# Reordering the features of a pairwise attention on the chip, and summing three score slots in ten

## The chip, the cores and the metric

The kernel runs on one core of a Trainium2 chip. A core has a matrix engine (PE, with a weight loader shown as PEld), a vector engine (DVE), an activation engine (ACT), a general engine (POOL) and a queue engine that issues most transfers (SP). Each runs its own list of instructions in order and waits on semaphores for the others. The metric is the time of one execution in microseconds of device time; lower is better.

## The reference, cut to what matters

x has 64 graphs of 256 nodes with 128 features, adj is one 256x256 matrix. Each of four layers normalizes x, applies relu and adds a graph block's result to x: a gated recurrent block of five steps, a polynomial block, a block with normalized rows, and a pairwise attention. The change touches the last:

```python
def _L3_gnn_ref(x, W, b_lin, a, bias):           # called with W = bias = adj
    W1, W2 = (W[:, :F], W[:, F:])
    s1 = jnp.einsum('bkf,ef->bke', x, W1)
    s2 = jnp.einsum('bkf,ef->bke', x, W2)
    pre = s1[:, :, None, :] + s2[:, None, :, :] + b_lin
    h = jnp.where(pre >= 0, pre, ALPHA * pre)
    e = jnp.einsum('bije,e->bij', h, a) + bias
    attn = jax.nn.softmax(e, axis=2)
    out = jax.nn.sigmoid(jnp.einsum('bij,bjf->bif', attn, x))
```

For every graph and every pair (i, j) of its nodes, 256 features e are passed through a leaky relu and summed with weights a[e]. That is 64 x 256 x 256 x 256 values, and most of the time goes there.

## The kernel before

**Fronts and tails.** The graphs are taken two at a time: 32 pairs. `front(p)` is the chain of all work of a pair up to its attention: the first three layers and then the projections s1 and s2 of the fourth, in two halves of 128 features each, already multiplied by 0.8 times the size of a: s1a and the negated s2 in a PSUM bank (`s2a`, copied to `s2c`) for the first half, s1b and `s2n` for the second. `front` also makes `lin`, the linear part of the score that depends on j alone: a product with `g2`, copied as `quarter`, written to DRAM and read back over all partitions by two transfers on SP (L635, L637). `tail(p, ic, ...)` takes the finished scores of 128 nodes i, adds adj (L679, DVE) and lin (L689, POOL), and does softmax, the product with x, the sigmoid and the store.

**Slots, halves, tiles.** The leaky relu is a linear part plus a relu, and relu(s1 + s2) = s1 - min(s1, -s2), so a half is a min, or a relu, of one column of s1 (fixed i) against a row of s2 (all j). A slot is four nodes i, 32 apart; a pair has 64 slots, and each slot has two halves. One half of one slot fills one tile `rl`, 128 features x 4 nodes x 2 graphs x 256 nodes j (128x2048). Three engines fill tiles, one whole tile each at a time, in `work_on_tile`: DVE takes the first half with one min of 2048 columns (L794); ACT takes the second half with eight relus of 256 columns (L808); POOL takes either half with eight instructions of 256 columns (L820), whose scalar s1 comes through one pointer while the other operand is a constant.

**Scoring and summing.** PE sums over the 128 features: `score` multiplies a tile with a 128x32 window of `win` or `win_n`, which holds a's sign in one column, so that the four nodes' sums go to four rows of a PSUM bank (four matmuls, L876). 64 such half-slots of tiles make a block of 128 nodes i. For one slot in four (`SHARE = (1, 4)`) the two halves are summed ahead of PE: DVE or POOL fills the first half, POOL fills the second half in a form with signs (L817: `s2z`, the second half's s2 times `rho`, the product of the two halves' signs, with two pointers `s1h` and `s1l` as lower and upper limits), and a transfer on POOL's queue adds the one tile into the other in SBUF (L837, 1 MB). PE then scores one tile in place of two. `s2z`, `s1h` and `s1l` are made in the front by POOL (L647) and DVE (L660, L661).

**Order.** Every engine's order is fixed when the program is built, by a planner at the end of the kernel: it holds a planned clock for each engine, takes the engine whose clock is lowest, and gives it the ready piece with the best rank: a tail's step first, then a front's step, then an add or a score, then a new tile. Planned durations stand in the code. There are 12 tiles; an engine may hold at most 8 (DVE), 3 (ACT) and 4 (POOL) at once. The set-up of constants is two such chains; the second, `other_constants`, runs beside the first front.

Of the kernel before, what the change touches and what calls it, by code (L numbers as in the profile page):

```python
# [8 lines left out]
F32 = mybir.dt.float32  # L9
# [15 lines left out]
SHARE = (1, 4)  # L25
# [6 lines left out]
def kernel(  # L32
# [87 lines left out]
    def take():  # L120

        spare.sort(key=lambda b: b[1])
        return spare.pop(0)
# [36 lines left out]
    make_identity(nc, ident)  # L160
    minus_half = const.tile([P, NB * NC], F32, name="minus_half")
# [43 lines left out]
    win = const.tile([P, NE, 63], F32, name="win")  # L205
    win_n = const.tile([P, NE, 63], F32, name="win_n")
    w1 = const.tile([P, N], F32, name="w1")
    w2n = const.tile([P, N], F32, name="w2n")
    g2 = const.tile([P, 32], F32, name="g2")
    signs = const.tile([P, NE + 2], F32, name="signs")  # L210
    rho, never = signs[:, NE:NE + 1], signs[:, NE + 1:NE + 2]
# [47 lines left out]
    def other_constants():  # L259
# [22 lines left out]
        a_rep = work.tile([P, NE, P], F32, name="a_rep", tag="short", bufs=12)  # L282
        nc.vector.memset(a_rep, 1.0)
        for k in range(NE):
            nc.vector.tensor_scalar(a_rep[:, k, :], a_rep[:, k, :], acol[:, k:k + 1], None, op0=OP.mult)
        t_a = ran(DVE, 0.9)
        yield DVE, clock[DVE]
        nc.vector.memset(win, 0.0)
        nc.vector.memset(win_n, 0.0)
        nc.vector.tensor_scalar(signs[:, 0:NE], acol, 0.0, None, op0=OP.is_ge)  # L290
        nc.vector.tensor_scalar(signs[:, 0:NE], signs[:, 0:NE], 2.0, -1.0, op0=OP.mult, op1=OP.add)
        nc.vector.tensor_mul(rho, signs[:, 0:1], signs[:, 1:2])
        nc.vector.tensor_scalar(never, rho, MOST_NEGATIVE, None, op0=OP.mult)
        size = work.tile([P, NE], F32, name="size")
        nc.vector.tensor_mul(size, acol, signs[:, 0:NE])
        nc.vector.tensor_scalar(size, size, 1.0 - ALPHA, None, op0=OP.mult)
        nc.vector.tensor_mul(blin_s, blin, size)
        adj_s = work.tile([P, NE, N], F32, name="adj_s", tag="short", bufs=12)
        for k in range(NE):
            nc.vector.tensor_copy(win[:, k, 31:32], signs[:, k:k + 1])  # L300
            nc.vector.tensor_scalar(win_n[:, k, 31:32], signs[:, k:k + 1], -1.0, None, op0=OP.mult)
            nc.vector.tensor_scalar(adj_s[:, k, :], adj_n[:, k, :], size[:, k:k + 1], None, op0=OP.mult)
        t = ran(DVE, 2.4)
        for c in range(NC):
            yield PE, t, 1
            b = take()
            for k in range(NE):
                nc.tensor.transpose(b[0][:, k * P:(k + 1) * P], adj_s[:, k, c * P:(c + 1) * P], ident)
            t = ran(PE, 0.4, t, b[1])
            yield DVE, t  # L310
            if c:
                nc.vector.tensor_scalar(w2n, b[0][:, 0:N], -1.0, None, op0=OP.mult)
            else:
                nc.vector.tensor_copy(w1, b[0][:, 0:N])
            t = ran(DVE, 0.35, t)
            spare.append([b[0], t])

        yield PE, t_a, 1
        b = take()
        for k in range(NE):  # L320
            nc.tensor.matmul(b[0][:, 0:P], adj_n[:, k, P:2 * P], a_rep[:, k, :], start=(k == 0), stop=(k == NE - 1))
        t = ran(PE, 0.8, t_a, b[1])
        yield DVE, t
        nc.vector.tensor_scalar(g2, b[0][:, 0:32], ALPHA, None, op0=OP.mult)
        t = ran(DVE, 0.25, t)
# [97 lines left out]
    def front(p):  # L423
# [201 lines left out]
        for g in range(4):  # L625
            nc.tensor.matmul(b[0][g * 32:(g + 1) * 32, 0:P], g2, flat(hT)[:, g * P:(g + 1) * P],
                             start=True, stop=True, skip_group_check=True)
        t = ran(PE, 0.22, t_hT, b[1])
# [3 lines left out]
        t = ran(ACT, 0.2, t)  # L632
# [3 lines left out]
        lin = feat("lin")  # L636
        nc.sync.dma_start(flat(lin).rearrange("p (q n) -> p q n", q=4), row[0:P:32, :].unsqueeze(0).to_broadcast([P, 4, P]))  # L637
        t_lin = moved(moved(t))
# [6 lines left out]
        yield POOL, t_2  # L645
        s2z = feat("s2z")
        nc.gpsimd.tensor_scalar(s2z, s2n, rho, 1.0, op0=OP.mult, op1=OP.mult)  # L647
        t_z = ran(POOL, 0.65, t_2)
# [9 lines left out]
        yield DVE, t_b  # L658
        s1h, s1l = feat("s1h"), feat("s1l")
        nc.vector.tensor_scalar(s1h, s1b, never, None, op0=OP.max)  # L660
        nc.vector.tensor_scalar(s1l, s1b, -1.0, never, op0=OP.mult, op1=OP.min)  # L661
        t_z = max(t_z, ran(DVE, 1.0, t_b))
# [9 lines left out]
        READY[p] = dict(x3=x3, h3=h3, hT=hT, s1=(s1a, s1b), s2a=by_feature(s2a), s2c=s2c, s2n=s2n, s2z=s2z, s1h=s1h, s1l=s1l,  # L672
                        lin=lin, t_lin=t_lin, since=(max(t_n, t_s2a), max(t_b, t_2), t_z))

    def tail(p, ic, pe, since, x3, h3):

        yield DVE, since
        sc = feat("sc", **SHORT)
        nc.vector.tensor_add(sc, by_feature(pe), adj_n[:, ic, :].unsqueeze(1).to_broadcast([P, NB, N]))  # L679
        t = t_pe[p * NC + ic] = ran(DVE, ELEMENTS, since)  # L680
        ops = READY[p]
# [53 lines left out]
    tiles = [[relu_pool.tile([P, 4, NB, N], F32, name=f"rl{k}", bufs=1), 0.0] for k in range(12)]  # L735
# [43 lines left out]
    def work_on_tile(e):  # L779
# [10 lines left out]
        if e == DVE:  # L790
            since = max(ops["since"][k], free)
            whole = [P, 4, NB, N]
            rows = ops["s1"][0][:, :, i0:i0 + 97:32].rearrange("p b g -> p g b").unsqueeze(3)
            nc.vector.tensor_tensor(t, rows.to_broadcast(whole), ops["s2a"].unsqueeze(1).to_broadcast(whole), op=OP.min)  # L794
            done = ran(DVE, 2.2, since)
            t_s2v[p % 2] = max(t_s2v[p % 2], done)
            parts = 1
        elif e == ACT:
            since = max(ops["since"][k], free)
            if "s2p" not in ops:  # L800
                ops["s2p"] = s2p
                nc.scalar.copy(s2p, ops["s2n"])
                ran(ACT, COPY, since)
            parts = 2
            for g in (2 * part, 2 * part + 1):
                for b in range(NB):
                    i = i0 + g * 32
                    nc.scalar.activation(t[:, g, b, :], s2p[:, b, :], AF.Relu, bias=ops["s1"][1][:, b, i:i + 1], scale=-1.0)  # L808
            done = ran(ACT, 1.43, since)
        else:  # L810
            since = max(ops["since"][k], free)
            parts = 4
            for b in range(NB):
                i = i0 + part * 32
                row = slice(i, i + 1)
                if k == 2:
                    nc.gpsimd.tensor_scalar(t[:, part, b, :], ops["s2z"][:, b, :], ops["s1h"][:, b, row], ops["s1l"][:, b, row],  # L817
                                            op0=OP.min, op1=OP.max)
                else:
                    nc.gpsimd.tensor_scalar(t[:, part, b, :], ops["s2n" if k else "s2c"][:, b, :], ops["s1"][k][:, b, row],  # L820
                                            MOST_NEGATIVE, op0=OP.min, op1=OP.max)
            done = ran(POOL, 1.06 if k == 2 else 0.9, since)
# [40 lines left out]
    def score(tile_):  # L863
# [10 lines left out]
        w = win[:, 1] if e == ACT else win_n[:, k % 2]  # L874
        for g in range(4):
            nc.tensor.matmul(pe[g * 32:(g + 1) * 32, :], w[:, 31 - r:63 - r], flat(t[:, g]),  # L876
                             start=first, stop=(left[block] == 0), skip_group_check=True)
# [118 lines left out]
```

## Time and profile before

| What | us |
|---|---|
| Median of three runs (4946.7 to 4952.7) | 4949.8 |
| The profiled execution | 4947.9 |
| Its span | 4946.1 |
| Idle time of PE in the span (4946.1 - 4800.8) | 145.3 |
| Idle time of DVE | 193.5 |
| Idle time of ACT | 221.1 |
| Idle time of POOL | 231.6 |
| Start of the first tile (timeline) | 121.9 |
| Adds on POOL's queue, median from issue to landing | 7.6 |

The page gives for each engine its busy time, which is the union of its instructions' intervals; consecutive instructions overlap, so the mean duration of one is more than what one more would cost. A group of instructions is one line, engine and operation with its tiles: how many, their busy time, the mean of one, and the idle time before them with what ended it. PE's records are matmul passes: a matmul in float32 has two. L12 is line 12 of the kernel. The chain that ended last follows the work back from the last instruction, at each step to what released it.

### The profile page before, as it was taken

To read this page: it belongs to the slowest core of one execution; us is meant where nothing else is said; L and a number is where in the kernel's file an instruction comes from. 1 tells how busy PE (TensorE), PEld (TensorE's weight loads), DVE (VectorE), ACT (ScalarE), POOL (GpSimd) and SP (SyncE) were. 2 spreads that over 40 slices of the span, in tenths; PEclk is the share of its full clock that TensorE was granted. 3 is DMA by queue.
4 is the path that set the end of the run, shared out by engine and by line. 5 is a ranking of instruction groups with operands and counts; after the bars stand their busy time and mean duration, and the time that the engine had idled before them with its cause. 6 is when DMAs were issued, how large, how long until landed. Compare 5 with 4: busy or idle time off the path is not lost.

```text
span 4946.1 us, 132376 instructions
## 1 busy us (share of the span) xinstructions
PE 4800.8 (97%) x51993; PEld 1737.4 (35%) x51993; DVE 4752.6 (96%) x3302; ACT 4725.0 (96%) x12361; POOL 4714.5 (95%) x8918
## 2 busy tenths in 40 slices
PE   7999999999999999999999999999999999999997
PEld 3333333333333333333333333333333333333322
DVE  3999999999999999999999999999999999999998
ACT  3999999999999999999999999999999999999998
POOL 1999999999999999999999999999999999999998
PEclk9999999999999999999999999999999999999999
DMA  0556555565555565555565555655555555555566
GB/s 20 111 117 126 117 109 119 116 125 119 119 117 119 116 125 118 118 114 114 118 123 120 117 116 118 124 117 117 120 117 118 121 118 116 117 118 117 122 125 125
DMA packets 134051, 573.96 MB, mean 116 GB/s; under 512 B 12720, under 2 KB 67888, under 8 KB 67888
## 3 DMA queue, kind: packets, MB, share of 16 engines
q0 software_dynamic: 73728, 536.90, 54.2%
q1 hardware_dynamic: 58976, 28.59, 2.3%
q8 instruction: 406, 6.65, 0.5%
q14 instruction: 221, 1.81, 0.1%
q10 hardware_dynamic: 720, 0.00, 0.0%
HBM read 18.09 MB, written 10.49 MB: 6 GB/s over the span
## 4 chain that ended last, share of the span: by engine, by line
PE 52%; DVE 19%; POOL 14%; issue 5%; DMA 5%; ACT 4%; POOLq 0%; ACTq 0%; DVEq 0%
PE bank L876 32%; PE bank L338 18%; DVE rl L794 15%; POOL rl L817 6%; DMA rl<-rl 5%; POOL rl L820 5%; ACT rl L808 3%; PE bank L366 2%; POOL rl L837 1%; POOL d L505 1%; DVE hT L512 1%; DVE bank L508 1%; PE bank L359 1%; POOL mv L333 0%; DVE rh L470 0%
## 5 line engine op out<-in xcount | busy, mean ns | idle before, releaser
L808 ACT ACTIVATE rl<-bank,s1b 128x256 f32<-128x256 f32 x10344 | 4199.2, 947 | 63.3 <-PE bank L876 46.1
L794 DVE TENSOR_TENSOR rl<-s1a,bank 128x2048 f32<-128x2048 f32 x1844 | 4120.1, 2275 | 46.0 <-PE bank L876 22.9
L876 PE MATMUL bank<-rl,win_n 128*32 128x512 f32 x18328 | 2290.8, 594 | 78.3 <-DVE rl L794 53.9
L817 POOL TENSOR_SCALAR rl<-s2z,s1h,s1l 128x256 f32<-128x256 f32 x4096 | 2228.1, 634 | 13.2 <-PE bank L876 7.6
L876 PE MATMUL bank<-rl,win 128*32 128x512 f32 x10344 | 1367.4, 594 | 0.0
L876 PEld LDWEIGHTS bank<-rl,win_n 128*32 128x32 f32 x18328 | 580.4, 110 | 1320.4 <-issue 981.5
L820 POOL TENSOR_SCALAR rl<-s2n,s1b 128x256 f32<-128x256 f32 x1944 | 890.0, 521 | 18.5 <-DMA rl<-rl 3.5
L820 POOL TENSOR_SCALAR rl<-s2c,s1a 128x256 f32<-128x256 f32 x1632 | 747.4, 523 | 8.8
L876 PEld LDWEIGHTS bank<-rl,win 128*32 128x32 f32 x10344 | 335.9, 110 | 667.2 <-issue 529.0
L837 POOL DMA_DIRECT2D rl<-rl x512 | 413.3, 810 | 20.9 <-DVE rl L794 15.8
L338 PE MATMUL bank<-mT,wts 128*32 128x512 f32 x2560 | 335.3, 592 | 0.6 <-DVE rh L470 0.6
L338 PE MATMUL bank<-adj_t,h 128*32 128x256 f32 x5120 | 310.1, 383 | 3.6 <-ACT h L524 3.6
L505 POOL TENSOR_TENSOR d<-d,hT 128x512 f32<-128x512 f32 x155 | 206.8, 1334 | 58.9 <-ACT d L501 58.9
L338 PEld LDWEIGHTS bank<-adj_t,h 128*32 128x32 f32 x5120 | 165.3, 111 | 170.5 <-issue 53.8
L408 ACT ACTIVATE h<-x,mv 128x128 f32<-128x128 f32 x384 | 186.8, 795 | 7.3 <-DVE mv L404 6.8
L414 ACT COPY mT<-bank 128x512 f32<-128x512 f32 x160 | 153.3, 961 | 41.4 <-PE bank L338 39.7
L466 ACT ACTIVATE bank<-bank,gate_b 128x512 f32<-128x512 f32 x160 | 160.1, 1001 | 18.3 <-PE bank L338 15.5
L489 ACT ACTIVATE bank<-bank,gate_b 128x512 f32<-128x512 f32 x160 | 168.8, 1055 | 7.5 <-PE bank L338 7.5
L338 PE MATMUL bank<-rh,u5t 128*32 128x512 f32 x1280 | 168.3, 593 | 5.9 <-DVE rh L470 5.8
L501 ACT ACTIVATE d<-bank,gate_b 128x512 f32<-128x512 f32 x155 | 165.4, 1067 | 7.0 <-PE bank L338 6.8
L338 PE MATMUL bank<-mT,w 128*32 128x512 f32 x1280 | 168.3, 593 | 0.0
L338 PE MATMUL bank<-hT,wts 128*32 128x512 f32 x1280 | 168.1, 593 | 0.0
(132 smaller groups left out, 3476.1 us busy)
## 6 DMA issues: line engine op xcount, KB each, us to landing
rl<-rl POOLq DMA_DIRECT2D x512, 1024.0 KB, 7.6
xin<-in_x_dram SPq DMA_DIRECT2D x64, 128.0 KB, 6.1
lin<-row SPq DMA_DIRECT2D x32, 256.0 KB, 8.0
out_dram<-o SPq DMA_DIRECT2D x64, 128.0 KB, 3.6
row<-quarter SPq DMA_DIRECT2D x32, 64.0 KB, 4.1
w_raw<-in_L_gnn_w_w_dram SPq DMA_DIRECT2D x3, 128.0 KB, 2.8
th_raw<-in_L_gnn_Theta_dram SPq DMA_DIRECT2D x1, 320.0 KB, 3.7
adj_n<-in_adj_dram SPq DMA_DIRECT2D x1, 256.0 KB, 3.3
```

Source lines behind the costliest of these rows:

```text
L338: nc.tensor.matmul(o[g:g + 32], w[:, g:g + 32], t, start=start, stop=stop, skip_group_check=True)
L408: nc.scalar.activation(h[:, k, :], s[:, k, :], AF.Relu, bias=mv[:, k, 0:1], scale=mv[:, k, 1:2])
L466: nc.scalar.activation(r[0], pr[0], AF.Tanh, bias=br, scale=0.5)
L489: nc.scalar.activation(pr[0], pr[0], AF.Tanh, bias=bz, scale=0.5)
L501: nc.scalar.activation(d, by_feature(pv[0]), AF.Tanh, bias=bh, scale=1.0)
L505: nc.gpsimd.tensor_sub(d, d, hT)
L794: nc.vector.tensor_tensor(t, rows.to_broadcast(whole), ops["s2a"].unsqueeze(1).to_broadcast(whole), op=OP.min)
L808: nc.scalar.activation(t[:, g, b, :], s2p[:, b, :], AF.Relu, bias=ops["s1"][1][:, b, i:i + 1], scale=-1.0)
L817: nc.gpsimd.tensor_scalar(t[:, part, b, :], ops["s2z"][:, b, :], ops["s1h"][:, b, row], ops["s1l"][:, b, row], op0=OP.min, op1=OP.max)
L820: nc.gpsimd.tensor_scalar(t[:, part, b, :], ops["s2n" if k else "s2c"][:, b, :], ops["s1"][k][:, b, row], MOST_NEGATIVE, op0=OP.min, op1=O ...
L837: nc.gpsimd.dma_start(out=t.rearrange("p g b n -> p (g b n)"), in_=z.rearrange("p g b n -> p (g b n)"), accum_op=OP.add)
L876: nc.tensor.matmul(pe[g * 32:(g + 1) * 32, :], w[:, 31 - r:63 - r], flat(t[:, g]), start=first, stop=(left[block] == 0), skip_group_check= ...
```

## The change

`other_constants` now sorts the 256 features on the chip: those with a >= 0 first in their order, then the others from the end. Two iotas, comparisons and small matmuls with ones give each feature a rank; a 0/1 matrix `moved_to` per half, made by comparing the rank with a counter, sends the feature of rank 2m to the first half and that of rank 2m + 1 to the second, both at place m. So partners in the two halves share the sign of a, but for one pair when the number of positive features is odd; the one feature that then stands alone with the other sign, `odd`, is taken out of the sorted weights and is worked on by itself. The transposes of adj that gave `w1` and `w2n` become matmuls with `moved_to`.

As partners share their sign, a summed second half needs no rho and no two limits: POOL fills it with the same one-pointer instruction as any other tile. `s2z`, `s1h` and `s1l` are gone, and `win` and `win_n` have one half only.

The odd feature is a term min(s2o, s1o) for each pair of nodes. `front` makes s2o together with lin (one more column in `g2`'s matmul, a second broadcast transfer, ahead of that of lin) and s1o by four matmuls of one column and one small activation. The tail's first instruction, DVE's sum with adj, becomes two instructions (one for each graph) that add min(s2o, s1o) to the bank; adj is instead put into the bank by PE, by matmuls with the identity ahead of a block's first score.

The share of summed slots goes from one in four to three in ten, and the number of tiles from 12 to 13.

```diff
-SHARE = (1, 4)
+SHARE = (3, 10)
...
+    place = work.tile([P, N], mybir.dt.int32, name="place", bufs=1)
+    nc.gpsimd.iota(place, pattern=[[1, N]], base=0, channel_multiplier=0)
+    feature = work.tile([P, NE], mybir.dt.int32, name="feature", bufs=1)
+    nc.gpsimd.iota(feature, pattern=[[P, NE]], base=0, channel_multiplier=1)
...
-    win = const.tile([P, NE, 63], F32, name="win")
-    win_n = const.tile([P, NE, 63], F32, name="win_n")
+    win = const.tile([P, 63], F32, name="win")
+    win_n = const.tile([P, 63], F32, name="win_n")
...
+    odd_one = const.tile([P, 34], F32, name="odd_one")
+    g2, w1_odd, b_odd = odd_one[:, 0:32], odd_one[:, 32:33], odd_one[:, 33:34]
...
+        nc.vector.tensor_scalar(rest, number, total, None, op0=OP.add)
+        nc.vector.tensor_sub(rest, rest, counted)
+        nc.vector.tensor_sub(rank, counted, rest)
+        nc.vector.tensor_mul(rank, rank, positive)
+        nc.vector.tensor_add(rank, rank, rest)
...
+        moved_to = work.tile([P, NE, NE, P], F32, name="moved_to", tag="short", bufs=12)
+        for k in range(NE):
+            nc.vector.tensor_scalar(moved_to[:, k].rearrange("p h m -> p m h"), placed.rearrange("p (m h) -> p m h", h=NE),
+                                    rank[:, k:k + 1], None, op0=OP.is_equal)
...
             for k in range(NE):
-                nc.tensor.transpose(b[0][:, k * P:(k + 1) * P], adj_s[:, k, c * P:(c + 1) * P], ident)
-            t = ran(PE, 0.4, t, b[1])
+                nc.tensor.matmul(b[0][:, 0:N], adj_s[:, k, c * P:(c + 1) * P], moved_to[:, k].rearrange("p h m -> p (h m)"),
+                                 start=(k == 0), stop=(k == NE - 1))
+            t = ran(PE, 1.2, t, b[1])
...
+            nc.tensor.matmul(b[0][:, P + g:P + g + 1], flat(hT)[:, g * P:(g + 1) * P], w1_odd, start=True, stop=True)
...
+        s1o = work.tile([P, NB * NC], F32, name="s1o")
+        nc.scalar.activation(s1o, b[0][:, P:P + NB * NC], AF.Identity, bias=b_odd, scale=1.0)
...
-        nc.sync.dma_start(flat(lin).rearrange("p (q n) -> p q n", q=4), row[0:P:32, :].unsqueeze(0).to_broadcast([P, 4, P]))
-        t_lin = moved(moved(t))
+        lin, s2o = feat("lin"), feat("s2o")
+        for k, o in enumerate((s2o, lin)):
+            nc.sync.dma_start(flat(o).rearrange("p (q n) -> p q n", q=4), row[1 - k:P:32, :].unsqueeze(0).to_broadcast([P, 4, P]))
+            t = moved(t)
+        t = moved(t)
+        t_lin = t
...
-        s2z = feat("s2z")
-        nc.gpsimd.tensor_scalar(s2z, s2n, rho, 1.0, op0=OP.mult, op1=OP.mult)
...
-        s1h, s1l = feat("s1h"), feat("s1l")
-        nc.vector.tensor_scalar(s1h, s1b, never, None, op0=OP.max)
-        nc.vector.tensor_scalar(s1l, s1b, -1.0, never, op0=OP.mult, op1=OP.min)
...
-        nc.vector.tensor_add(sc, by_feature(pe), adj_n[:, ic, :].unsqueeze(1).to_broadcast([P, NB, N]))
-        t = t_pe[p * NC + ic] = ran(DVE, ELEMENTS, since)
+        for b in range(NB):
+            nc.vector.scalar_tensor_tensor(sc[:, b, :], ops["s2o"][:, b, :], ops["s1o"][:, b * NC + ic:b * NC + ic + 1],
+                                           by_feature(pe)[:, b, :], op0=OP.min, op1=OP.add)
+        t = t_pe[p * NC + ic] = ran(DVE, 0.8, since, ops["t_lin"])
...
-    tiles = [[relu_pool.tile([P, 4, NB, N], F32, name=f"rl{k}", bufs=1), 0.0] for k in range(12)]
+    tiles = [[relu_pool.tile([P, 4, NB, N], F32, name=f"rl{k}", bufs=1), 0.0] for k in range(13)]
...
-                if k == 2:
-                    nc.gpsimd.tensor_scalar(t[:, part, b, :], ops["s2z"][:, b, :], ops["s1h"][:, b, row], ops["s1l"][:, b, row],
-                                            op0=OP.min, op1=OP.max)
-                else:
-                    nc.gpsimd.tensor_scalar(t[:, part, b, :], ops["s2n" if k else "s2c"][:, b, :], ops["s1"][k][:, b, row],
-                                            MOST_NEGATIVE, op0=OP.min, op1=OP.max)
-            done = ran(POOL, 1.06 if k == 2 else 0.9, since)
+                nc.gpsimd.tensor_scalar(t[:, part, b, :], ops["s2n" if k else "s2c"][:, b, :], ops["s1"][min(k, 1)][:, b, row],
+                                        MOST_NEGATIVE, op0=OP.min, op1=OP.max)
+            done = ran(POOL, 0.9, since)
...
-        w = win[:, 1] if e == ACT else win_n[:, k % 2]
+        if first:
+            for b in range(NB):
+                side_by_side(by_feature(pe)[:, b, :], ident, adj_n[:, ic, :], b == 0, False)
+            ran(PE, 0.87, since, t_pe.get(block - 2, 0.0))
+        w = win if e == ACT else win_n
         for g in range(4):
             nc.tensor.matmul(pe[g * 32:(g + 1) * 32, :], w[:, 31 - r:63 - r], flat(t[:, g]),
-                             start=first, stop=(left[block] == 0), skip_group_check=True)
+                             start=False, stop=(left[block] == 0), skip_group_check=True)
```

## The prediction

> **What bounds the kernel now.** I read the busy line of the page first, then the chain that ended last, the costliest groups, the windows by stage, the timeline and the waits. The profiled execution took 4947.9 us (span 4946.1); the median of the three timed runs is 4949.8, so a sum made against the one is good for the other within 2 us.
>
> ```profile
> PE 4800.8 (97%) x51993; PEld 1737.4 (35%) x51993; DVE 4752.6 (96%) x3302; ACT 4725.0 (96%) x12361; POOL 4714.5 (95%) x8918
> ...
> PE 52%; DVE 19%; POOL 14%; issue 5%; DMA 5%; ACT 4%; POOLq 0%; ACTq 0%; DVEq 0%
> PE bank L876 32%; PE bank L338 18%; DVE rl L794 15%; POOL rl L817 6%; DMA rl<-rl 5%; POOL rl L820 5%; ACT rl L808 3%; PE bank L366 2%; POOL rl L837 1%; POOL d L505 1%; DVE hT L512 1%; DVE bank L508 1%; PE bank L359 1%; POOL mv L333 0%; DVE rh L470 0%
> ```
>
> All four engines are nearly full, and the chain is shared: PE holds 52% of it, the three engines that fill score tiles (DVE, ACT, POOL: the producers) 37%, the summing DMA 5%. So neither a cut of PE alone nor of the producers alone is worth its whole size. The windows show where each rules (columns: stretch, length, busy time of PE, PEld, DVE, ACT, POOL, clock, DMA share):
>
> ```profile
> 0.00:50.00 50.00, 39.81 (x361) 16.44 (x365) 20.52 (x63) 17.57 (x30) 4.49 (x11) 0.97 0.15 38
> ...
> 1000.00:2000.00 1000.00, 984.13 (x10684) 353.18 (x10680) 984.43 (x671) 981.95 (x2582) 986.52 (x1869) 1.00 0.59 120
> ...
> 4800.00:4850.00 50.00, 43.55 (x392) 11.52 (x388) 50.00 (x26) 50.00 (x142) 49.07 (x96) 1.00 0.64 130
> ```
>
> The first 125 us are set-up and the first front, with the producers mostly idle; the last 246 us have the producers full and PE at about 84%. Between them all are at 97 to 99%. The granted clock is 1.00 there, so it plays no part.
>
> The prices come from these groups (busy, mean ns of one):
>
> ```profile
> L808 ACT ACTIVATE rl<-bank,s1b 128x256 f32<-128x256 f32 x10344 | 4199.2, 947 | 63.3 <-PE bank L876 46.1
> L794 DVE TENSOR_TENSOR rl<-s1a,bank 128x2048 f32<-128x2048 f32 x1844 | 4120.1, 2275 | 46.0 <-PE bank L876 22.9
> L817 POOL TENSOR_SCALAR rl<-s2z,s1h,s1l 128x256 f32<-128x256 f32 x4096 | 2228.1, 634 | 13.2 <-PE bank L876 7.6
> L820 POOL TENSOR_SCALAR rl<-s2n,s1b 128x256 f32<-128x256 f32 x1944 | 890.0, 521 | 18.5 <-DMA rl<-rl 3.5
> L820 POOL TENSOR_SCALAR rl<-s2c,s1a 128x256 f32<-128x256 f32 x1632 | 747.4, 523 | 8.8
> L837 POOL DMA_DIRECT2D rl<-rl x512 | 413.3, 810 | 20.9 <-DVE rl L794 15.8
> ```
>
> Instructions overlap their neighbours, so the price of one more is busy time over count, not the mean: ACT 4199.2/10344 = 0.406 us, DVE 4120.1/1844 = 2.234, POOL with two pointers 2228.1/4096 = 0.544, with one 1637.4/3576 = 0.458, an add issued by POOL 413.3/512 = 0.807. PE's ends are modelled; its price is the distance between starts:
>
> ```profile
> 2500.57 1.91 PE L338 MATMUL bank<-adj_t,h 128*32 128x256 f32 x32
> 2502.30 1.90 PE L876 MATMUL bank<-rl,win_n 128*32 128x512 f32 x16
> 2504.01 1.04 PE L876 MATMUL bank<-rl,win 128*32 128x512 f32 x8
> 2504.87 1.04 PE L876 MATMUL bank<-rl,win_n 128*32 128x512 f32 x8
> ```
>
> Scoring one tile is 8 records in 0.86 us (2504.01 to 2504.87); 32 records of 256 columns take 1.73 us (2500.57 to 2502.30).
>
> **The change part by part.** There are 2048 slots with two halves each. The built program has 614 summed slots instead of 512, so 4096 - 614 = 3482 tiles to score instead of 3584. Its counts: DVE fills 1814 tiles (1844 before), ACT issues 10128 activations (10344), POOL 8128 one-pointer instructions instead of 4096 with two and 3576 with one.
>
> *PE.* 102 fewer scores x 0.86 = -87.7 us. New: at each of 64 blocks adj goes into the bank by 8 matmuls of 256 columns, 16 records, 1.73/2 = 0.865, so +55.4. New too: 128 matmuls of one column with 128x128 weights, 256 records. No row shows one; below, they hide (0); above, each costs a weight load as in the transposes of hT (67.7 us over 640 loads = 0.106), 27.1. They are mostly weight load and go in fours, partly overlapped: I take 13.5. Sum -18.8 (-32 to -5).
>
> *DVE.* 30 fewer tiles: -67.0. The two preparations of a front and the old tail sum go:
>
> ```profile
> L660 DVE TENSOR_SCALAR s1h<-s1b,signs 128x512 f32<-128x512 f32 x32 | 38.2, 1192 | 13.1 <-ACT s1b L655 13.1
> L661 DVE TENSOR_SCALAR s1l<-s1b,signs 128x512 f32<-128x512 f32 x32 | 20.7, 647 | 0.0
> L679 DVE TENSOR_TENSOR sc<-bank,adj_n 128x512 f32<-128x512 f32 x64 | 43.6, 681 | 12.1 <-PE bank L876 11.9
> ```
>
> That is -58.9 and -43.6. In its place come 128 three-operand instructions of 256 columns. Rows of that operation: 128 columns 342 ns (L600), 512 columns 679 ns (L470); on the line between them 454 ns, so +58.1 (43.8 at the one end, 86.9 at the other). Sum -111.4 (-126 to -83). On splitting one instruction in two, the Trainium skill, "VectorE: DVE Perf Modes", section on the TRN2 errata, says that each instruction pays a fixed extra time and gives a measured fixed term of about 150 cycles: an estimate by that page is 0.156 us for each of the 64 added instructions, 10 us. The rows' own line has a larger fixed part, 342 - 112 = 230 ns, 14.7 us; it is already in the 58.1 and the rows decide.
>
> *ACT.* 216 fewer activations: -87.7. One 128x4 activation for each of 32 pairs is new: at most the 128x128 copy of L631, 0.735, 23.5; at least nothing, where it overlaps its neighbours; I take 12. Sum -76 (-88 to -64).
>
> *POOL.* -2228.1 - 1637.4 + 8128 x 0.458 = -142.9; the s2z preparation (L647) goes, -22.1; 102 more adds x 0.807 = +82.3. Sum -83 (up to -44 if an added issue takes the longest seen, 1.192).
>
> *Summing DMA.* Its queue is busy 54.2% of 4946 us for 512 adds, 5.24 us each; 102 more are +534 us, 66% of a shorter span. As long as an add lands before its tile is due, that costs nothing; the cover is the other tiles already made, now of 13 instead of 12. The Trainium skill, "DMA: Bandwidth & Descriptors", section on the anatomy of one SWDGE DMA, fits 2.0 us plus bytes over 436 GB/s: by that, an estimate of 4.4 us for 1 MB against 7.6 from issue to landing here, with 2.4 of transfer against 5.24, and the queue would stand at 30%. An adding transfer is slower than the fit, so I keep the row.
>
> *Moves that hide.* One more broadcast per pair stands ahead of lin on SP: 0.36 us to issue and 8.0 to land. The first pair's lin was issued at 120.2 us and its first tail began at 210.1; the cover is some 80 us, and without it every DVE tile behind the tail's first instruction would be late. The two iotas stand on POOL where it works 4.5 us of 50; the nearest row, an affine select, takes 0.3. The set-up has about 13 more small DVE instructions of 0.15 to 0.35 us in the stage in which the first front runs through DVE, and PE hops between: +3 us (0 to 8), all on the path.
>
> **The sum.** Weighted by the chain's shares of 4946 us: PE 2572 x 18.8/4801 = -10.1; DVE 940 x 111.4/4753 = -22.0; POOL 692 x 83/4715 = -12.2; ACT 198 x 76/4725 = -3.2; set-up +3. Total -44: 4903 us. That is cautious: where PE ruled for want of tiles, better supplied producers shorten it too. If the producers ruled throughout, the least of their cuts would come whole: -76 + 3, 4875. PE sets how near: outside the first 125 and last 246 us it was busy 4495 of 4575 us, 98.3%. Less 19, that work fits in 4523 us at 99%, and 99.5% were reached in single windows of 100 us. 4523 + 371 + 2 gives 4896. I take **4893**, between the weighted sum and the producers' bound, near PE at 99%.
>
> **Rivals.**
> *Producers rule, PE follows: 4875* (4855 to 4882). For it: they are full in the last 246 us, and the waits for a free tile may shrink with the 13th. Against: PE would have to reach 99.4%.
>
> *PE becomes the bound: 4926* (4912 to 4945). If PE stays at 98.3% in the middle, 4476/0.983 + 371 + 2 = 4926. For it: 52% of the chain, and PE gains least of all. Against: its idle time was mostly lack of tiles.
>
> *Adds land late, slower: about 5010.* The place is the tile that waits for an add:
>
> ```profile
> PEld bank L876 <- DMA rl<-rl: 54.5, 63, 3.9
> ...
> PE bank L876 <- DMA rl<-rl: 23.1, 25, 3.3
> ...
> DVE rl L794 <- DMA rl<-rl: 17.7, 14, 3.9
> ...
> ACT rl L808 <- DMA rl<-rl: 11.6, 9, 2.4
> ```
>
> The chain gives the adds 5%, 247 us, 0.48 us each. At 0.6 us each, 614 cost 368, so +121 against the -55 that I forecast: 5014. It decides from 302/614 = 0.49 us on. For it: the queue rises from 54% to 66%, and landings up to 14.2 us are seen. Against: the idle time that names adds is little over 100 us in all, and a tile more is there.
>
> *The change doesn't do what it says:* the counts above rule that out for the sums and the pointers; left is a one-pointer price that doesn't hold for three quarters of POOL's tiles. At 0.468 instead of 0.458 (8128 x 0.010 = 81) POOL gains nothing, and as the tiles are dealt out in advance the others wait for it: near 4945.
>
> **How the numbers follow.** Forecast 0.45, producers' bound 0.20, PE's bound 0.20, late adds 0.10, pointer price 0.05. A measurement of this kernel tells 0.2%, 10 us, from no change. Faster by more takes in the first three nearly whole: 0.82; the same 0.07 (from the last, and the ends of PE's bound and of late adds); slower 0.11. The range runs from 4855, where all producers' gains come and some waits go, to 4942; it leaves out late adds and little else. The forecast's own range is 4882 to 4912.
>
> **What would show it.** One-pointer POOL instructions at 0.45 to 0.46 us busy each; PE busy near 4780 us, at or over 99% in the middle windows; PE's share of the chain above 52%; waits on "DMA rl<-rl" not far above 110 us; the DMA queue at 65 to 66%; the tail's new DVE instruction near 450 ns and the one-column matmuls under 27 us. The prediction is wrong if the middle windows show PE below 98% while the producers wait for tiles or adds, or if PE's new matmuls cost more than the 32 us by which scoring outweighs the adj matmuls.

## The result, and the profile after

The changed kernel takes 5003.6 us (median of four runs, 4996.8 to 5014.3) against 4951.2 before on the same chip: a ratio of 1.0108, 95% interval 1.0084 to 1.0132. It is slower by 1.1%, where 4893 us, 1.2% faster, was forecast. The profiled execution took 4997.0 us, its span 4995.2.

The page of the changed kernel: busy time of each engine, the adds' queue (packets, MB, share), the chain that ended last.

```profile
PE 4851.9 (97%) x52487; PEld 1789.2 (36%) x52487; DVE 4659.2 (93%) x3289; ACT 4664.4 (93%) x12177; POOL 4662.2 (93%) x9446
...
q0 software_dynamic: 88416, 643.86, 64.2%
...
PE 55%; POOL 13%; DVE 13%; DMA 7%; ACT 7%; issue 4%; POOLq 0%; ACTq 0%; DVEq 0%
```

Two things differ from the forecast at once. The producers (the three engines that fill tiles) did lose work, 52 to 93 us each, but they are at 93% where they were at 95 to 96: they wait. And PE, which should have lost 19 us, has 51 us more. Its idle time in the span is what it was, 143.3 us against 145.3, so from the page alone PE's added work could be the whole loss; the runs below tell otherwise. The groups say where (busy, mean ns of one, idle before with what ended it):

```profile
L853 DVE TENSOR_TENSOR rl<-s1a,bank 128x2048 f32<-128x2048 f32 x1814 | 4060.1, 2277 | 173.7 <-PE bank L935 79.7 <-DMA rl<-rl 76.8 <-ACT s1a L726 14.1
L875 POOL TENSOR_SCALAR rl<-s2n,s1b 128x256 f32<-128x256 f32 x6256 | 2949.0, 659 | 113.2 <-DMA rl<-rl 59.9 <-PE bank L935 21.5 <-ACT s1b L717 13.5
L892 POOL DMA_DIRECT2D rl<-rl x614 | 567.8, 935 | 38.2 <-DVE rl L853 14.2 <-issue 13.2 <-POOL rl L875 7.5
L738 DVE SCALAR_TENSOR_TENSOR sc<-s2o,s1o,bank 128x256 f32<-128x256 f32 x128 | 55.3, 472 | 9.6 <-PE bank L935 9.6
L686 PE MATMUL bank<-hT,odd_one 128*32 128x128 f32 x256 | 52.3, 287 | 0.0
L688 PE MATMUL bank<-odd_one,hT 128*128 128x1 f32 x256 | 49.8, 264 | 0.0
```

DVE's idle time before a tile went from 46.0 to 173.7 us. L686 is the product that the trace of before has at L626, the same 256 records:

```profile
L626 PE MATMUL bank<-hT,g 128*32 128x128 f32 x256 | 13.5, 278 | 0.0
```

It took 13.5 us there and takes 52.3 here, beside 49.8 for the new one-column matmuls of L688. The timeline of PE in one front (start, length, then the group) shows why:

```profile
2817.48 0.38 PE L686 MATMUL bank<-hT,odd_one 128*32 128x128 f32 x2
2817.80 0.38 PE L688 MATMUL bank<-odd_one,hT 128*128 128x1 f32 x2
2818.11 0.41 PE L686 MATMUL bank<-hT,odd_one 128*32 128x128 f32 x2
2818.44 0.38 PE L688 MATMUL bank<-odd_one,hT 128*128 128x1 f32 x2
```

A matmul with 32 output rows and one with 128 alternate, four times. Each starts some 0.32 us after the one ahead of it, where four of 32 rows used to run side by side: the whole step takes 2.57 us per front, measured to the start of the next work, against 0.22 before. That is 2.35 x 32 = 75 us.

The other half, the waiting, is not spread evenly. Waits for adds (us in total, times, longest):

```profile
DVE rl L853 <- DMA rl<-rl: 76.8, 28, 7.9
POOL rl L875 <- DMA rl<-rl: 66.9, 18, 7.8
ACT rl L867 <- DMA rl<-rl: 46.0, 21, 6.2
PEld bank L935 <- DMA rl<-rl: 34.2, 34, 3.6
PE bank L935 <- DMA rl<-rl: 21.6, 20, 4.9
```

Together they are 245 us, where the waits for adds came to 113 before, and single waits of 8 us stand where the longest was 3.9. One such place, in windows of 10 us (stretch, length, busy time of PE, PEld, DVE, ACT, POOL, clock, DMA share, GB/s), and two lines of its timeline:

```profile
2820.00:2830.00 10.00, 10.00 (x114) 3.92 (x117) 9.01 (x7) 9.70 (x27) 9.92 (x20) 1.00 0.29 59
2830.00:2840.00 10.00, 9.32 (x104) 3.18 (x100) 3.57 (x3) 9.60 (x24) 8.08 (x17) 1.00 0.96 206
2840.00:2850.00 10.00, 6.79 (x64) 2.19 (x60) 10.00 (x6) 6.49 (x17) 5.27 (x12) 0.92 0.75 154
```

```profile
2839.48 8.88 DVE L853 TENSOR_TENSOR rl<-s1a,bank 128x2048 f32<-128x2048 f32 x4 [6.43 <-DMA rl<-rl]
...
2844.73 3.61 POOL L875 TENSOR_SCALAR rl<-s2n,s1b 128x256 f32<-128x256 f32 x8 [6.47 <-DMA rl<-rl]
```

At 2823.3 and 2823.8 SP issued the broadcasts of s2o and lin; at 2823.4, 2827.6 and 2833.9 POOL issued adds. Those three landed after 16.0, 17.0 and 16.0 us, while the adds ahead of them took 7.0 to 7.5. By the DMA's packet records, no packet of the first add began before 2829, some 6 us after its issue, though the DMA engines were busy for 29% of that window; an add issued away from the fronts, with no add ahead of it, has its first packet after 1.4 us (median of 263). Then three adds went through one after another, at a full queue, and DVE, POOL and in the end PE (a pause of 3.2 us) stood still for tiles.

The list of transfers of the changed kernel (KB each, median us from issue to landing; POOL, with its adds, issues more transfers here than SP):

```profile
rl<-rl POOLq DMA_DIRECT2D x614, 1024.0 KB, 8.0
...
s2o<-row SPq DMA_DIRECT2D x32, 256.0 KB, 8.6
lin<-row SPq DMA_DIRECT2D x32, 256.0 KB, 11.0
```

It is so at most fronts: at 27 of the 32 an add needs more than 10 us to land. Counted over the trace, adds issued between 6 us before and 14 us after a front's write of `row` landed after 11.75 us on average (84 adds), all others after 8.20; before the change 8.71 (66 adds) and 7.80. In the 35 us behind the issue of each write of `row`, a quarter of the time, lie 146 of the 225 us that DVE is idle between 130 and 4700 us; before it was 31 of 93.

### The profile page after: what moved, and what is told of

Same layout as the page of the kernel before. It is cut to its first block, busy times and chain, and to the rows that moved or that the text cites. A ratio compares the mean times of both kernels' runs of the same rounds, so it can differ in the third digit from the quotient of the medians.

```text
span 4995.2 us, 134047 instructions
## 1 busy us (share of the span) xinstructions
PE 4851.9 (97%) x52487; PEld 1789.2 (36%) x52487; DVE 4659.2 (93%) x3289; ACT 4664.4 (93%) x12177; POOL 4662.2 (93%) x9446
## 3 DMA queue, kind: packets, MB, share of 16 engines
q0 software_dynamic: 88416, 643.86, 64.2%
## 4 chain that ended last, share of the span: by engine, by line
PE 55%; POOL 13%; DVE 13%; DMA 7%; ACT 7%; issue 4%; POOLq 0%; ACTq 0%; DVEq 0%
PE bank L935 32%; PE bank L398 19%; DVE rl L853 11%; POOL rl L875 10%; DMA rl<-rl 7%; ACT rl L867 5%; PE bank L426 2%; POOL rl L892 1%; PE bank L419 1%; POOL d L565 1%; DVE hT L572 1%; DVE bank L568 1%; PE bank L688 1%; PE bank L686 1%; ACT h L468 0%
## 5 line engine op out<-in xcount | busy, mean ns | idle before, releaser
L853 DVE TENSOR_TENSOR rl<-s1a,bank 128x2048 f32<-128x2048 f32 x1814 | 4060.1, 2277 | 173.7 <-PE bank L935 79.7
L867 ACT ACTIVATE rl<-bank,s1b 128x256 f32<-128x256 f32 x10128 | 4045.9, 757 | 144.8 <-PE bank L935 94.6
L875 POOL TENSOR_SCALAR rl<-s2n,s1b 128x256 f32<-128x256 f32 x6256 | 2949.0, 659 | 113.2 <-DMA rl<-rl 59.9
L935 PE MATMUL bank<-rl,win_n 128*32 128x512 f32 x17728 | 2227.4, 596 | 57.4 <-DVE rl L853 34.7
L935 PE MATMUL bank<-rl,win 128*32 128x512 f32 x10128 | 1335.5, 595 | 0.0
L875 POOL TENSOR_SCALAR rl<-s2c,s1a 128x256 f32<-128x256 f32 x1872 | 895.6, 655 | 14.3 <-DMA rl<-rl 7.0
L892 POOL DMA_DIRECT2D rl<-rl x614 | 567.8, 935 | 38.2 <-DVE rl L853 14.2
L561 ACT ACTIVATE d<-bank,gate_b 128x512 f32<-128x512 f32 x155 | 145.3, 937 | 22.6 <-PE bank L398 22.4
L526 ACT ACTIVATE bank<-bank,gate_b 128x512 f32<-128x512 f32 x160 | 138.3, 864 | 20.4 <-PE bank L398 19.5
L398 PEld LDWEIGHTS bank<-mT,wts 128*32 128x32 f32 x2560 | 83.6, 110 | 193.8 <-issue 152.1
L549 ACT ACTIVATE bank<-bank,gate_b 128x512 f32<-128x512 f32 x160 | 146.7, 917 | 6.7 <-PE bank L398 6.7
L474 ACT COPY mT<-bank 128x512 f32<-128x512 f32 x160 | 127.5, 797 | 26.1 <-PE bank L398 25.8
```

The source lines that it names most:

```text
L398: nc.tensor.matmul(o[g:g + 32], w[:, g:g + 32], t, start=start, stop=stop, skip_group_check=True)
L474: nc.scalar.copy(c, by_feature(bank[0]))
L526: nc.scalar.activation(r[0], pr[0], AF.Tanh, bias=br, scale=0.5)
L549: nc.scalar.activation(pr[0], pr[0], AF.Tanh, bias=bz, scale=0.5)
L561: nc.scalar.activation(d, by_feature(pv[0]), AF.Tanh, bias=bh, scale=1.0)
L892: nc.gpsimd.dma_start(out=t.rearrange("p g b n -> p (g b n)"), in_=z.rearrange("p g b n -> p (g b n)"), accum_op=OP.add)
```

## The experiments

Three theories were set against each other; A and B before the first four runs, C after them. A: PE is the bound, and its 75 us of alternating matmuls are the loss. B: 102 more adds fill the queue by themselves, anywhere. C: the second broadcast in 512-byte pieces holds up the adds near each front. Ratios are to the kernel before on the same chip, with 95% intervals; the chips differ by up to 0.5%, so ratios are compared and not times.

**Without the one-column matmuls.**

```diff
-            nc.tensor.matmul(b[0][:, P + g:P + g + 1], flat(hT)[:, g * P:(g + 1) * P], w1_odd, start=True, stop=True)
-        nc.scalar.activation(s1o, b[0][:, P:P + NB * NC], AF.Identity, bias=b_odd, scale=1.0)
+        nc.scalar.activation(s1o, b[0][:, 0:NB * NC], AF.Identity, bias=b_odd, scale=1.0)
```

> Leaves out the four one-column matmuls of each front (s1o is then made from the other product's columns); every other instruction and every engine's order are those of the changed kernel. Theory A, PE is the bound and the one-column matmuls hold it 2.57 - 0.22 = 2.35 us more for each of 32 pairs, 75 us: 4997 falls by 55 to 75 us, to 4922 to 4942, and PE's records of the 128-column product go from 52 us busy back to about 14. Theory B, the 102 more adds land late and starve the tiles: hardly any change, 4980 to 4997, and the waits on the adds stay above 200 us.

Measured: 1.0062 (1.0045 to 1.0078). PE's busy time fell by 50 us, to 4802.0, but the time only by 0.5%, where 1.1 to 1.5% was expected of theory A, and the named waits for adds rose to 325 us. Theory A alone falls: PE with 50 us less to do stands still more. The 0.5% is a part of the loss all the same. PE's pauses had a price of their own: in the middle (130 to 4700 us) the clock was granted at half speed in 15 stretches, each behind a pause of PE of some 2 us or more, for 61 us in all, against 27 us in the changed kernel and none before.

**The four products first, then the four one-column matmuls.**

```diff
         for g in range(4):
             nc.tensor.matmul(b[0][g * 32:(g + 1) * 32, 0:P], g2, flat(hT)[:, g * P:(g + 1) * P],
                              start=True, stop=True, skip_group_check=True)
+        for g in range(4):
             nc.tensor.matmul(b[0][:, P + g:P + g + 1], flat(hT)[:, g * P:(g + 1) * P], w1_odd, start=True, stop=True)
```

> The same matmuls, but the four products of 32 output rows stand together and the four one-column ones behind them. Theory A, with the cost in the switching between the two shapes: the four products take 0.22 us again, the eight one-column records about 0.11 to 0.13 us each, 1.2 to 1.3 us in place of 2.57, so 32 x 1.3 = 42 us off PE and 4950 to 4965. If the weight load is the cost and not the switching: 4985 or more. Theory B: no change.

Measured: 1.0085 (1.0069 to 1.0101). The step took 1.31 us in place of 2.57, as expected of the switching, and the time hardly followed: 0.6 to 0.9% was expected, and the interval overlaps that of the changed kernel. PE's busy time fell by 10 us and not by 42, with 72 us of the middle at half clock, and the waits for adds rose to 307 us.

**One slot in four.**

```diff
-SHARE = (3, 10)
+SHARE = (1, 4)
```

> The changed kernel with one slot in four summed, as before the change; planned anew. Theory A: 102 more tiles to score, +88 us on a PE that is the bound, while the producers have time to spare: 5040 to 5085. Theory B: the adds' queue goes back to 54%, waits on the adds fall to about 100 us, and the time falls to 4900 to 4950.

Measured: 1.0007 (0.9998 to 1.0017), between the two expectations. Its busy line and chain:

```profile
PE 4898.0 (99%) x53303; PEld 1807.3 (36%) x53303; DVE 4668.3 (94%) x3297; ACT 4645.0 (93%) x12073; POOL 4606.5 (93%) x9384
...
PE 84%; DVE 9%; POOL 3%; issue 2%; DMA 2%; ACT 0%; DVEq 0%; ACTq 0%; POOLq 0%
```

Here PE is the bound, almost never idle, as theory A has it; but the kernel is faster than with three in ten, where A gave a slower one. Theory B gave about 100 us of waits for adds, as the adds' queue went back to 53.6%. They stayed at 225 us, most of them here:

```profile
POOL rl L875 <- DMA rl<-rl: 126.7, 31, 6.0
DVE rl L853 <- DMA rl<-rl: 73.5, 38, 3.3
```

Adds near a front still land after 10.8 us, the others after 7.85. So the late adds come with a queue that is no fuller than before, which speaks against B. They cost little here: PE is idle for only 13 us of the middle (130 to 4700 us), against 81 with three in ten.

**The planner told the step's true length.**

```diff
-        t = ran(PE, 0.6, t_hT, b[1])
+        t = ran(PE, 2.57, t_hT, b[1])
```

> The changed kernel, with the planner told 2.57 us in place of 0.6 for the step with the one-column matmuls. If the 75 us are a cost as such (theory A): within 15 us of 4997. If the harm comes from an order made for a cheaper step, with tiles and adds late against the plan: 4940 to 4970. Theory B: no change.

Measured: 1.0217 (1.0199 to 1.0235), outside all expectations: a truer plan for PE gave a worse order, with 394 us of named waits for adds. Why this order starves more stays open; the run shows that the order alone, with the same work, can be worth a per cent. The runs below with one in four, with adj on DVE or with twelve tiles are planned anew too, so that a difference of a few tenths of a per cent there can be the order's; the others keep the order of the kernel that they start from.

**Without the second broadcast.**

```diff
-        lin, s2o = feat("lin"), feat("s2o")
+        lin = s2o = feat("lin")
         for k, o in enumerate((s2o, lin)):
-            nc.sync.dma_start(flat(o)...
+            if k:
+                nc.sync.dma_start(flat(o)...
```

> Leaves out the second broadcast of each front (the tail's DVE instruction reads lin in place of s2o); engines' order as in the changed kernel. Theory C, the second broadcast of 512-byte pieces holds the DMA engines, the adds issued meanwhile land at 12.2 us in place of 8.2, their tiles come free late and all engines starve behind every front: adds that meet a broadcast go back to about 9 us, DVE's idle time in the middle from 225 to under 150 us, and the ratio to the kernel before from 1.011 to 0.998 to 1.003. Theory B, 102 more adds fill the queue by themselves, at any time: the ratio stays at 1.007 to 1.011. Theory A, PE's one-column matmuls: no change either.

Measured: 0.9990 (0.9980 to 1.0000). Adds near a front land after 10.2 us (11.75 with both broadcasts), DVE is idle 191 us of the middle (225): less of a fall than expected for both, but the time went where theory C put it, and the waits for adds fell from 245 to 136 us. One transfer fewer per front brings the kernel back to the time of the one before, and B and A, which gave no change here, fall as the main cause.

**One contiguous broadcast.**

```diff
-        row = dram.tile([P, P], F32, name="row", bufs=2)
-        nc.sync.dma_start(row, quarter)
-        lin, s2o = feat("lin"), feat("s2o")
-        for k, o in enumerate((s2o, lin)):
-            nc.sync.dma_start(flat(o)..., row[1 - k:P:32, :].unsqueeze(0).to_broadcast([P, 4, P]))
-            t = moved(t)
+        row = dram.tile([2, 4, P], F32, name="row", bufs=2)
+        for k in range(2):
+            nc.sync.dma_start(row[k], quarter[k:P:32, :])
+            t = moved(t)
+        rows = work.tile([P, 2, NB, N], F32, name="rows")
+        nc.sync.dma_start(rows..., row.rearrange("k g n -> (k g n)").unsqueeze(0).to_broadcast([P, 8 * P]))
+        lin, s2o = rows[:, 0], rows[:, 1]
```

> The same results of s2o and lin by another way: the eight rows that are wanted are written to one contiguous piece of DRAM (two small transfers) and come back in one broadcast of 4 KB per partition in place of two with four 512-byte pieces each. The bytes broadcast are the same, 512 KB a front. Theory C with the number of small pieces as the cause: the broadcast lands in under 6 us, overlapping adds under 10 us, ratio 0.997 to 1.003. If the bytes are the cause: adds still at 12 us, ratio 1.007 to 1.011. Theory B: 1.007 to 1.011.

Measured: 0.9912 (0.9897 to 0.9926), better than expected: the first broadcast, or the write of all 64 KB of `quarter`, had a price too. Adds near a front land after 9.0 us. Chain and some waits of this version:

```profile
PE 67%; DVE 10%; POOL 9%; ACT 7%; issue 3%; DMA 3%; ACTq 0%; POOLq 0%; DVEq 0%
```

```profile
PEld bank L936 <- DMA rl<-rl: 26.1, 26, 3.5
...
DVE rl L854 <- DMA rl<-rl: 9.1, 13, 1.7
```

The waits for adds are 78 us in all, below those of the kernel before, with the same 614 adds in the queue (65.4% of the time). The same bytes are broadcast, in pieces of 4 KB in place of 512 bytes; the run does not tell the pieces apart from the smaller write.

**And the one-column matmuls in the products' shape.**

```diff
-            nc.tensor.matmul(b[0][:, P + g:P + g + 1], flat(hT)[:, g * P:(g + 1) * P], w1_odd, start=True, stop=True)
+        for g in range(4):
+            side_by_side(b[0][:, P + g:P + g + 1], flat(hT)[:, g * P:(g + 1) * P], w1_odd)
```

> The last one and, besides, the one-column matmuls as 32-row pieces of the same shape as the four products, which they follow, so that PE does not switch shapes: the step should take about 0.9 us in place of 2.57, 53 us off PE in all. Without starving, PE's share counts again (theory A beside C): 0.988 to 0.996. If only starving decides, as the run without the columns suggests: the same as the run with one broadcast, within 0.2%.

Measured: 0.9863 (0.9848 to 0.9877). Two groups of this version, the new columns and the old products:

```profile
L398 PE MATMUL bank<-odd_one,hT 128*32 128x1 f32 x1024 | 14.6, 172 | 0.0
L686 PE MATMUL bank<-hT,odd_one 128*32 128x128 f32 x256 | 13.2, 279 | 0.0
```

Four times as many matmuls take 14.6 us in all in place of 49.8, and the products are back at 13.2. The step takes 0.52 us. PE lost 54.6 us against the run before it, as expected, and the time fell by 24 us, 0.5%, to a little below the expected range. That is half of what PE saved, and as much as the run without the columns gained while adds were late. So the one-column matmuls cost some 0.5% in either case; repairing the broadcast did not make PE's work count for more.

**Both repairs with one slot in four.**

> The last one with one slot in four summed. The run with one in four alone had PE busy 4898 us of 4971 and PE in 84% of its chain, so PE was its bound: 53 us off PE give 0.988 to 0.993. If more sums pay once adds are not held up, this is slower than the same with three in ten, by up to 1%.

Measured: 0.9854 (0.9840 to 0.9869), 4900.0 us against 4970.4: faster than both kernels, below the expected 0.988, and no different from three in ten within the intervals.

```profile
PE 4835.1 (99%) x54071; PEld 1776.1 (36%) x54071; DVE 4660.8 (95%) x3297; ACT 4634.8 (95%) x12073; POOL 4607.1 (94%) x9384
...
PE 93%; DVE 2%; DMA 2%; ACT 1%; POOL 1%; issue 1%; SPq 0%; ACTq 0%; POOLq 0%; DVEq 0%
```

PE is now simply full. The gain of the repaired change does not need more sums: one slot in four does as well. How the rest of the gain divides between the one-pointer instruction, the 13th tile and the transfers, no run takes apart but for the broadcast of lin, in the next run.

**The kernel before with a contiguous broadcast of lin.**

```diff
-        row = dram.tile([P, P], F32, name="row", bufs=2)
-        nc.sync.dma_start(row, quarter)
+        row = dram.tile([4, P], F32, name="row", bufs=2)
+        nc.sync.dma_start(row, quarter[0:P:32, :])
         lin = feat("lin")
-        nc.sync.dma_start(flat(lin)..., row[0:P:32, :].unsqueeze(0).to_broadcast([P, 4, P]))
+        nc.sync.dma_start(flat(lin), row.rearrange("g n -> (g n)").unsqueeze(0).to_broadcast([P, 4 * P]))
```

> The kernel before, with its one broadcast (lin) made contiguous in the same way: 2 KB per partition in one piece in place of four of 512 bytes. There the adds near a front land at 8.7 us against 7.8 elsewhere, and the idle time near the broadcasts is some 20 us an engine. Theory C says that a single broadcast is mostly covered: 0.995 to 1.000. If it were worth as much as in the changed kernel, 0.99 or less.

Measured: 0.9964 (0.9952 to 0.9976). One broadcast in pieces, with the write ahead of it, cost the kernel before 0.4%. Its traces show where: adds near a front land after 7.97 us in place of 8.71, and the waits for adds fall from 113 to 80 us.

**adj back on DVE**, in the versions with one in four and three in ten:

```diff
-            nc.vector.scalar_tensor_tensor(sc[:, b, :], ...
+            nc.vector.scalar_tensor_tensor(by_feature(pe)[:, b, :], ...
...
+        nc.vector.tensor_add(sc, by_feature(pe), adj_n[:, ic, :].unsqueeze(1).to_broadcast([P, NB, N]))
...
-        if first:
-            for b in range(NB):
-                side_by_side(by_feature(pe)[:, b, :], ident, adj_n[:, ic, :], b == 0, False)
...
-                             start=False, stop=(left[block] == 0), skip_group_check=True)
+                             start=first, stop=(left[block] == 0), skip_group_check=True)
```

> The version with both repairs and one slot in four, with adj added by DVE as before (an instruction more in each tail, 64 x 0.68 = 43 us on DVE) in place of PE's matmuls with the identity (64 x 0.865 = 55 us off PE). PE had 93% of the chain there, so theory A holds for that version: 0.974 to 0.980. If DVE's 43 us take back what PE gains: 0.985.

> The same with three slots in ten. PE had 58% of the chain and the producers 35%: if more sums pay once adds aren't held up, 0.974 to 0.981 and not slower than one in four; if the 102 adds cost as much as they spare, 0.980 to 0.988.

Measured: 0.9871 (0.9855 to 0.9888) and 0.9914 (0.9900 to 0.9929). At one in four nothing is gained: PE lost 26 us of busy time, not 55, and fell from 93% to 52% of its chain, the others took its place. At three in ten it is slower than with adj on PE, and than either expectation. In both versions all four engines are busy for 95 to 98% of the span, so work moved from one to another finds no idle one; the new order may have its part.

**Twelve tiles** in the changed kernel:

```diff
-... for k in range(13)]
+... for k in range(12)]
```

> The changed kernel with 12 tile buffers. If the 13th covers late adds (theory C, with fewer tiles every late add starves sooner): 1.015 to 1.03. If it does nothing: 1.009 to 1.012, the ratio of the changed kernel.

Measured: 1.0152 (1.0137 to 1.0167). With twelve tiles the loss is 0.4% larger, at the lower edge of what was expected if the 13th covers late adds. As the order is planned anew, the run does not show that the tile itself is worth that; it does show that the 13th tile did not cause the loss.

## Why the prediction was wrong

**The step that failed** is the first of "Moves that hide": "One more broadcast per pair stands ahead of lin on SP", hidden by 80 us of cover. The cover was asked for the broadcast's own reader, the tail, and that reader never waited for it. What the broadcast shares with others, the DMA engines through which the adds go, was not asked. Taking that transfer alone away moves the ratio from 1.0108 to 0.9990, so of the 2.2% between forecast and result 1.2% lie there. A second step failed beside it, the 13.5 us for the one-column matmuls in PE's sum: they cost 75 us of PE, and 0.5% of the time.

The prediction named two signs of being wrong. The second came, new matmuls on PE over 32 us. The first did not, narrowly: PE is busy for 98.2% of the middle as a whole, although the producers wait for adds.

**The rival that came true** had 0.10. "Adds land late, slower: about 5010" named the right wait and nearly the right time, but put it down to the queue's share. With a contiguous broadcast the same queue stands at 65.4% and the waits go below those of before; with one slot in four it stands at 53.6% and they stay at 225 us. So the share alone does not make them. The 0.48 us of chain for each add was right as a scale: 7% of 4995 us over 614 adds is 0.57, and the rival decided from 0.49 on. That its time came out so near is in part luck, as it counts PE as 19 us lighter where PE was 51 us heavier.

**PE's sum** failed in one term. Scores and adj came near their prices (95 us less and 68 us more busy time, for 87.7 and 55.4); the one-column matmuls were bounded by a weight load each, 0 to 27 us, and cost 75, because they also stopped the products beside them from overlapping. The rows I took the price from were of one shape each. The Trainium skill, "TensorEngine Tiling (Array Packing)", section Key Properties, says that changing the tiling mode drains the engine; the alternation above agrees, at about 0.32 us for each change and its two records, and the run in one shape removed it. PE's measured 51 us more is this sum, -87.7 + 55.4 + 75 = 43, and the 27 us of the middle at half clock, which lengthen its records by up to 14 us (an estimate, half of 27); in the run with one broadcast, whose middle has no half clock, PE has 38 us more than before.

**What held.** The tail's new DVE instruction: 55.3 us, 472 ns, forecast 58.1 and 454. The queue: 64.2%, forecast 65 to 66. DVE's cut: 93 us, short of the 111 but in its range of 83 to 126. The set-up: the first tile starts at 129 us in place of 122, at the upper end of 0 to 8. Less held on the other two producers. ACT's cut was 61 us, below its range of 64 to 88. POOL's one-pointer instruction starts 0.448 us after the one ahead of it, as before; but by the prediction's measure, busy time over count, it came out at (2949.0 + 895.6)/8128 = 0.473, above the 0.468 at which the prediction let POOL gain nothing, and an issued add at 567.8/614 = 0.925 us in place of 0.807. These records overlap (together they cover 4156 us, added up they are 4412), so busy time over count overstates them; POOL's cut was 52 us instead of 83. One step of the sum is off by 2 us (4476/0.99 is 4521 and not 4523), and nothing rests on it.

**The weighing** of PE's bound against the producers' bound assumed that one of them would rule. In the changed kernel neither did: of the 133 us that DVE's idle time in the middle grew by, 115 lie in the quarter of the time behind the fronts, where the engines that fill tiles, and PE less, waited for the same late adds. With the transfers and the columns repaired, three in ten gives 0.9863, beside the 0.989 (4893 to 4949.8) that was forecast, but that it is so near is luck in two ways. The same broadcast of lin repaired gives 0.9964 for the kernel before, a gain that the forecast did not hold; against that kernel some 1.0% is left (an estimate, 0.9863/0.9964). And one slot in four does as well, so the added sums, from which PE's part of the forecast came, are not shown to be worth anything.

**Left open:** why the truer plan was the worst, whether the pieces or the smaller write freed the adds, and by what means a broadcast holds an add back.

## What to carry to other kernels

Ask of an added transfer not only whether its reader can wait, but which transfers in flight it delays; look at the landing times of the others near it, and split them into near and far, since a median over all (8.0 against 7.6 here) hides it. Here the broadcasts in small pieces were repaired by laying the source out contiguously first, with a smaller write. Give the kernel before the same repair, or its worth is counted as the change's. On PE, price a new matmul by what it does to its neighbours: keep one shape together, or give the small one the shape of those around it.

## What the runs showed of the hardware

Beside two broadcasts of 256 KB in 512-byte pieces, an add of 1 MB began some 6 us after its issue, where 1.4 us is usual, while the DMA engines were 29% busy and moved 59 GB/s; in the next 10 us they moved 206. So it did not wait for want of bandwidth; what it waited for, the runs do not show. Full-height and 32-row matmuls in alternation take about 0.32 us for each matmul (two records), while eight records of 32 rows run side by side in 0.22 us.

The granted clock follows PE's pauses. Between 130 and 4700 us of the changed kernel eight pauses of 2.1 to 3.2 us end in a stretch of 3.4 us at half clock; three others of 2.4 to 3.0 us do not. The kernel before has no pause over 2.2 us there and no such stretch. The Trainium skill, "TensorE: Matmul & The Clock Gate", section "What's actually happening", describes half rate after an idle window of about 3.4 us. The half rate agrees; the pauses measured here were shorter than that, and most of them were enough. In the run without the one-column matmuls, 61 us at half clock in place of 27 can have cost PE at most 17 us (an estimate, half of the 34 us), a part of what that run gave back.
